# Sums by node in a graph kernel on Trainium2: one-hot matrices stationary instead of gathered rows, and row weights multiplied by ScalarE

## The chip, the cores and the metric

The kernel runs on one NeuronCore of a Trainium2 chip (trn2). The metric is the device time of the whole kernel in microseconds (us). Before the change the median of three runs is 7461.32 us (7460.88 to 7475.34).

## What is computed

The input is a graph of 12500 nodes with 256 features each and 212500 edges (200000 drawn ones and one loop for each node), sorted by destination. Four layers follow one another, each added to its input, each on the layer-normalized input: a relational graph sum, a feed-forward layer on the half of the nodes that a router scores highest, a graph attention sum with 4 heads of 64 columns, and a mixture of 8 experts of which each node takes two. The change is in the two sums. Cut to them:

```python
# relation sum (8 relations, block-diagonal weights 32x32)
msg = h[edge_src] * edge_norm[:, None]
agg = segment_sum(msg, edge_rel * N + edge_dst, num_segments=R * N)
out = einsum('rnbi,rbio->nbo', agg.reshape(R, N, 8, 32), W)
...
# attention sum
alpha = leaky_relu(a_src[src] + a_dst[dst], 0.2)
ex = exp(alpha - segment_max(alpha, dst)[dst])
w = ex / segment_sum(ex, dst)[dst]
agg = segment_sum(xp[src] * w[..., None], dst)
x = x + elu(agg.reshape(n, 256) + bias)
```

## The kernel before, in words

The kernel has one path for graphs whose edges lie evenly over the nodes, taken here (`even`, line 926), and a general path that is not run. The stages, with their stretches in the profile:

- **Preparation and table** (0 to 480 us). The edges are laid out in tiles of 128 (1661 tiles), their destinations are checked, and `lcC` gets each edge's destination relative to the first node of its tile's window. STEPS (line 299) fixes that first node for every tile t in advance: 16 times a step, moving by 241/512 of a step a tile, so about 7.5 nodes. A window is WIN = 96 nodes. Then every node's layer-normalized row times each of the 8 relations' weights is written to a table T0 in HBM, so that the relation sum needs only one row of 256 for each edge.
- **Relation sum and feed-forward** (480 to 2920 us, `even_depths`, line 936). For each tile GpSimd (POOL) gathers 128 rows of T0 with an indirect DMA (`gather`, line 233; buffers `row`, 16 of them). VectorE (DVE) makes a one-hot matrix S of 128 edges x 96 nodes for six tiles at once (`one_hot`, line 919) and multiplies it by the edge weights (line 1017). TensorE (PE) adds row-half x S into two banks of PSUM (`windows`, line 892; the matmul is line 913): the gathered half row, 128 edges x 128 features, is the stationary operand, S streams, and the sum comes out as features x nodes, 512 nodes to a bank ("bin"), features 0 to 127 in one bank and 128 to 255 in the other. A window that crosses the edge of a bin takes a matmul in each. When the last tile of a bin is through, `summed` (line 956) copies both banks (ScalarE one, DVE the other), transposes them back to nodes x features (PE, line 967), adds x, and goes on through layer norm, router score and feed-forward for these 512 nodes (lines 972 to 1009), in small pieces between the sums of the next nodes.
- **Choice of the top half and tables for the attention** (2920 to 3220 us).
- **Attention sum and router** (3220 to 6110 us, `even_gat`, line 1070). Rows of 260 (256 features and 4 scores) are gathered (`fetch`, line 1143; buffers of six tiles, 12 of them). For groups of 30 tiles (GS) the scores become softmax weights w (`scores`, `sources`, `softmax`, lines 1181 to 1244). DVE multiplies six tiles of rows by w at once (`weigh`, line 1249, instruction line 1253) and makes S (line 922). PE adds as before (line 913). `summed` (line 1109) does bias and ELU in features x nodes, transposes back (line 1128), adds the node's row, and `route` (line 673) normalizes, scores the experts, and scatters each node's row to its two experts' lists: 8 indirect DMAs on POOL for 512 nodes (line 740).
- **Experts** (6110 to 7439 us, `slots`, line 818). Not touched.

The order of PE, DVE, ScalarE (ACT) and SyncE (SP) instructions within the two sums is written out by a planner (class `Plan`, line 50). Step t is the step of tile t's gather. Each piece of work is put at a step, pieces of a step run in the order in which they were put, and a generator's `yield n` puts its next piece n steps later. In the relation sum S of six tiles is at t - 8 and the use at t + 3; in the attention sum S is at 12, `weigh` at 17 and the first use at 19 steps after the group's end. `queue` lets one block of nodes start only when the one before is through; `follow` doesn't wait. Every engine runs its list strictly in that order. POOL's gathers run ahead until no buffer is free.

Of the kernel before, what the change touches and what calls it, by code (L numbers as in the profile page):

```python
# [34 lines left out]
P = 128  # L36
# [8 lines left out]
BIN = 512  # L45
GS = 30
SUB = 6

# [52 lines left out]
def gnn_ffn_kernel(ctx: ExitStack, tc: tile.TileContext, x, src, dst, etype, eweight, w_rel, wr, br,  # L101
# [29 lines left out]
    def bcast(ap1d, n):  # L131
# [35 lines left out]
                   allow_small_or_imprecise_dtypes=True)  # L167
    ident = const.tile([P, P], F32, name="ident")
# [137 lines left out]

    def tiles_of(t):
        return t.rearrange("q (c j) -> q c j", j=P)
# [10 lines left out]
    with ExitStack() as pre:  # L319
# [63 lines left out]
        for i, (t, nat, around, dt) in enumerate(((NS, KSN, 0.0, F32), (NBR, NBN, -FAR, F32), (DM, DMN, 0.0, BF16))):  # L383
# [26 lines left out]
                                       accum_out=viol[:, 3:4])  # L410
        total = pp.tile([P, 1], F32, name="total")
# [240 lines left out]
    def router(st):  # L652
# [20 lines left out]
        def route(ms, xg, wk, pst, psy, psc, behind=None):  # L673
# [6 lines left out]
            xe = wk.tile([P, 4, D + 1], F32, name="xe", bufs=3)  # L680
# [66 lines left out]
            o = wk.tile([P, 4, D], F32, name="o")  # L747
            for i, m in enumerate(ms):
                pt = pst[0].tile([P, 2, P], F32, name=pst[1])
                transpose(pt[:NE, 0, :], mk[:, i, :])  # L750
                yield 1
                mT = wk.tile([NE, P], F32, name="mT")
                nc.scalar.activation(mT, pt[:NE, 0, :], AF.Copy)
                yield 1
                pb = psy[0].tile([P, D], F32, name=psy[1])
                nc.tensor.matmul(pb, mT, b2s, start=True, stop=True)
                yield 2
                nc.vector.tensor_tensor(o[:, i, :], pb, xg[:, i, :], op=OP.add)
                n = rows(m)
                nc.sync.dma_start(O2[m * P:m * P + n, :], o[:n, i, :])  # L760
# [131 lines left out]
    def windows(psA, done):  # L892


        zeros = const.tile([1, BIN], BF16, name="zeros")
        nc.vector.memset(zeros, 0.0)
        NBIN = -(-NM * P // BIN)
        last = {}
        for t in range(NT):
            for b in range(STEPS[t] * 16 // BIN, (STEPS[t] * 16 + WIN - 1) // BIN + 1):  # L900
                last[b] = t
        open_ = {}

        def add(t, lhs, S):
            base = STEPS[t] * 16
            for b in range(base // BIN, (base + WIN - 1) // BIN + 1):
                if b not in open_:
                    open_[b] = [psA.tile([P, BIN], F32, name=f"bin{k}") for k in range(2)]
                    for a in open_[b]:
                        nc.tensor.matmul(a, zeros[:, :P], zeros, start=True, stop=False)  # L910
                lo, hi = max(base, b * BIN), min(base + WIN, (b + 1) * BIN)
                for k in range(2):
                    nc.tensor.matmul(open_[b][k][:, lo - b * BIN:hi - b * BIN], lhs(k), S[:, lo - base:hi - base],  # L913
                                     start=False, stop=last[b] == t)
# [4 lines left out]
    def one_hot(wk, lcC, t, n, **kw):  # L919

        S = wk.tile([P, SUB, WIN], F32, name="S", **kw)
        nc.vector.tensor_tensor(S[:, :n], lcC[:, t:t + n, None].to_broadcast([P, n, WIN]),  # L922
                                col[:, None, :WIN].to_broadcast([P, n, WIN]), op=OP.is_equal)
        return S

    def even():
        with ExitStack() as ev:
# [3 lines left out]
            nc.sync.dma_start(lcC, LCC)  # L931
            even_depths(AD, lcC)
# [3 lines left out]
    def even_depths(AD, lcC):  # L936


        with ExitStack() as md:
# [8 lines left out]
            with ExitStack() as r1:  # L948
                wk = r1.enter_context(tc.tile_pool(name="r1_w", bufs=1))
                rw = r1.enter_context(tc.tile_pool(name="r1_r", bufs=16))  # L950
                psA = r1.enter_context(tc.tile_pool(name="r1_pa", bufs=2, space=PSUM))
# [3 lines left out]

                def summed(b, sums):
                    ms = [m for m in range(b * BIN // P, (b + 1) * BIN // P) if m < NM]
                    G = len(ms)
                    xg = wk.tile([P, 4, D], F32, name="xg")
                    load_nodes(xg, x, ms, nc.sync)  # L960
                    aT = wk.tile([P, 2, BIN], F32, name="aT")
                    nc.scalar.activation(aT[:, 0, :G * P], sums[0][:, :G * P], AF.Copy)
                    nc.vector.tensor_copy(aT[:, 1, :G * P], sums[1][:, :G * P])
                    yield 3
                    for i, m in enumerate(ms):
                        pt = pst.tile([P, 2, P], F32, name="pt")
                        for k in range(2):
                            transpose(pt[:, k, :], aT[:, k, i * P:(i + 1) * P])
                        yield 3
                        nc.vector.tensor_tensor(X[:, m, :], xg[:, i, :], pt.rearrange("p k j -> p (k j)"), op=OP.add)  # L970
# [40 lines left out]
                add = windows(psA, lambda b, sums: plan.queue(line, plan.now + 1, summed(b, sums)))  # L1011
                rows_, S_ = {}, {}

                def matrices(j):
                    n = min(SUB, NT - j * SUB)
                    S = one_hot(wk, lcC, j * SUB, n, bufs=4)
                    nc.vector.tensor_tensor(S[:, :n], S[:, :n],
                                            ewC[:, j * SUB:j * SUB + n, None].to_broadcast([P, n, WIN]), op=OP.mult)
                    S_[j] = S
# [4 lines left out]

                def use(t):
                    g = rows_.pop(t)
                    add(t, lambda k: g[:, k * P:(k + 1) * P], S_[t // SUB][:, t % SUB, :])

                for t in range(NT):
                    if t % SUB == 0:  # L1030
                        plan.put(t - 8, lambda j=t // SUB: matrices(j))
                    plan.put(t, lambda t=t: fetch(t))
                    plan.put(t + 3, lambda t=t: use(t))
# [36 lines left out]
    def even_gat(AD, lcC):  # L1070

        with ExitStack() as ga:
# [25 lines left out]
            psA = ga.enter_context(tc.tile_pool(name="ga_pa", bufs=2, space=PSUM))  # L1098
# [4 lines left out]
            biasC = wp.tile([P, 2, 2], F32, name="biasC")  # L1103
            nc.sync.dma_start(biasC[:, :, 0], bias.rearrange("(k p) -> p k", p=P))
            nc.vector.tensor_scalar(biasC[:, :, 1], biasC[:, :, 0], -1.0, None, op0=OP.mult)

            plan = Plan()

            def summed(b, sums):
                ms = [m for m in range(b * BIN // P, (b + 1) * BIN // P) if m < NM]  # L1110
                G = len(ms)
                xg = wk.tile([P, 4, D], F32, name="xg")
                load_nodes(xg, X2, ms, nc.sync)
                u = wk.tile([P, 2, BIN], F32, name="u", bufs=1)
                en = wk.tile([P, 2, BIN], F32, name="en", bufs=1)
                for k in range(2):
                    s_, e_ = sums[k][:, :G * P], en[:, k, :G * P]
                    nc.scalar.activation(e_, s_, AF.Relu, scale=-1.0, bias=biasC[:, k, 1:2])
                    nc.vector.tensor_scalar(u[:, k, :G * P], s_, biasC[:, k, 0:1], 0.0, op0=OP.add, op1=OP.max)
                    yield 1  # L1120
                nc.scalar.activation(en[:, :, :G * P], en[:, :, :G * P], AF.Exp, scale=-1.0)
                yield 2
                nc.vector.tensor_tensor(u[:, :, :G * P], u[:, :, :G * P], en[:, :, :G * P], op=OP.add)
                yield 2
                for i, m in enumerate(ms):
                    pt = pst.tile([P, 2, P], F32, name="pt")
# [553 lines left out]
```

## Time and profile before

| What | Value |
|---|---|
| Median of three runs | 7461.32 us |
| The profiled execution | 7440.8 us, of it 7439.0 from the first to the last instruction |
| Granted TensorE clock, mean over the span | 0.719 |
| PE busy | 5498.0 us (74%) |
| PE weight loads busy (PEld) | 4635.6 us (62%) |
| DVE busy | 2928.5 us (39%) |
| ACT busy | 745.9 us (10%) |
| POOL busy | 4095.7 us (55%) |

A line of the profile's groups has the kernel's line, the engine, the operation, output and inputs by name with their shapes, the count, then the busy time and the mean in ns of one, and then the engine's idle time just before them with what ended most of it. In the timeline the first two columns are the start and the duration in us. An f32 matmul stands in the trace as two instructions, so 7700 records of line 913 in each stage are 3850 matmuls. Ends of matmuls are modelled; starts are not.

### The profile page before, as it was taken

How to read it: one execution, taken by the hardware profiler on the slowest of the kernel's cores; microseconds unless marked ns; L12 is line 12 of the kernel's file. 1: busy time of each engine (PE TensorE's matmuls, PEld its weight loads, DVE VectorE, ACT ScalarE, POOL GpSimd, SP SyncE). 2: the span in 40 equal slices, each digit the busy share in tenths (PEclk: the TensorE clock that was granted, in tenths of full speed). 3: DMA queues.
4: the chain of work that ended last, by engine and by line, in shares of the span. 5: the costliest groups of instructions: out<-in, count | busy, mean ns of one | idle time of the engine just before them, and what ended most of it. 6: DMA issues, size and time to landing. Idle time of an engine off the chain costs nothing. (4 is left out here: it accounts for less than half of the span.)

```text
span 7439.0 us, 75728 instructions
## 1 busy us (share of the span) xinstructions
PE 5498.0 (74%) x26987; PEld 4635.6 (62%) x26987; DVE 2928.5 (39%) x7669; ACT 745.9 (10%) x1537; POOL 4095.7 (55%) x3768
## 2 busy tenths in 40 slices
PE   7967888887788887537777776767867775777775
PEld 3446667666677766427666676766766764666654
DVE  6633222323332222745556565565554650111110
ACT  2310000000000000110000000000000001112111
POOL 0036666666666664047777777777777742222222
PEclk9977787877778888765555555565555557888887
DMA  7753333333333332444444444444444425555555
GB/s 253 300 202 96 102 100 101 100 98 100 101 101 102 102 101 68 150 133 119 123 120 120 124 121 122 124 119 121 122 121 116 126 77 173 138 137 142 137 136 158
DMA packets 437371, 949.39 MB, mean 128 GB/s; under 512 B 84371, under 2 KB 293222, under 8 KB 410783
## 3 DMA queue, kind: packets, MB, share of 16 engines
q0 software_dynamic: 199872, 494.39, 25.6%
q1 hardware_dynamic: 237108, 450.03, 19.4%
q8 instruction: 217, 3.56, 0.2%
q14 instruction: 174, 1.42, 0.1%
HBM read 617.71 MB, written 228.88 MB: 114 GB/s over the span
## 5 line engine op out<-in xcount | busy, mean ns | idle before, releaser
L234 POOL DMA_INDIRECT rows<-T1A,srcC x1661 | 1867.0, 1124 | 684.0 <-issue 455.5
L234 POOL DMA_INDIRECT row<-T,rowC x1661 | 1655.5, 997 | 847.8 <-issue 327.2
L913 PE MATMUL bin<-S,rows 128*128 128x96 f32 (+5 forms) x7700 | 1724.1, 391 | 340.5 <-issue 235.6
L913 PEld LDWEIGHTS bin<-S,rows 128*128 128x128 f32 x7700 | 1604.1, 304 | 444.5 <-issue 315.6
L913 PEld LDWEIGHTS bin<-S,row 128*128 128x128 f32 x7700 | 1232.5, 241 | 237.4 <-issue 221.1
L913 PE MATMUL bin<-S,row 128*128 128x96 f32 (+5 forms) x7700 | 1248.7, 322 | 98.9 <-issue 94.0
L882 POOL DMA_INDIRECT O<-y,toI x210 | 326.7, 1556 | 907.0 <-DVE y L881 419.1
L872 PE MATMUL ph<-xT,we 128*128 128x256 f32 x1680 | 469.7, 442 | 267.7 <-DVE xT L191 262.8
L922 DVE TENSOR_TENSOR S<-lcC,col 128x576 f32<-128x576 f32 x554 | 415.9, 751 | 440.8 <-PE bin L913 175.8
L872 PEld LDWEIGHTS ph<-xT,we 128*128 128x128 f32 x1680 | 372.7, 227 | 344.0 <-DVE xT L191 275.6
L993 PE MATMUL ph<-xT,w1s 128*128 128x512 f32 (+1 forms) x800 | 426.1, 663 | 132.9 <-ACT hT L995 68.6
L1253 DVE TENSOR_TENSOR rows<-rows,w 128x1536 f32<-128x1536 f32 x277 | 484.8, 1750 | 79.6 <-issue 60.9
L861 DVE CAST toI<-xs 128x2 int32<-128x2 f32 x105 | 17.7, 169 | 1024.6 <-DMA O<-y,toI 820.9
L878 PE MATMUL py<-we,hT 128*128 128x256 f32 x1680 | 381.1, 379 | 5.7 <-DVE y L881 5.7
L1001 PE MATMUL pt<-w2s,hT 128*128 128x256 f32 x1568 | 378.5, 385 | 3.2 <-issue 3.1
L469 PE MATMUL pm<-BD,xT 128*128 128x512 f32 x784 | 351.1, 601 | 12.8 <-ACT xT L189 12.3
L878 PEld LDWEIGHTS py<-we,hT 128*128 128x128 f32 x1680 | 318.8, 190 | 50.9 <-DVE y L881 7.7
L195 PE MATMUL pt<-ident,xn 128*128 128x128 f32 x588 | 121.7, 317 | 289.1 <-DVE xn L219 176.0
L993 PEld LDWEIGHTS ph<-xT,w1s 128*128 128x128 f32 x800 | 153.9, 213 | 254.6 <-issue 180.4
L1001 PEld LDWEIGHTS pt<-w2s,hT 128*128 128x128 f32 x1568 | 284.7, 191 | 36.1 <-issue 4.5
L189 ACT ACTIVATE xT<-pt 128x256 f32<-128x256 f32 x301 | 115.2, 383 | 1840.2 <-PE pt L195 979.6
L195 PEld LDWEIGHTS pt<-ident,xn 128*128 128x128 f32 x588 | 79.9, 164 | 342.1 <-issue 317.2
(267 smaller groups left out, 4893.5 us busy)
## 6 DMA issues: line engine op xcount, KB each, us to landing
we<-Wall SPq DMA_DIRECT2D x105, 1026.0 KB
T<-tb SPq DMA_DIRECT2D x97, 1024.0 KB
dmB<-DMN SPq DMA_DIRECT2D x277, 192.0 KB
xs<-XS SPq DMA_DIRECT2D x105, 257.0 KB
row<-T,rowC POOLq DMA_INDIRECT x1661
rows<-T1A,srcC POOLq DMA_INDIRECT x1661
xg<-in_x_dram SPq DMA_DIRECT2D x48, 512.0 KB
T1A<-t SPq DMA_DIRECT2D x97, 130.0 KB
```

What stands on the lines that cost most here:

```text
L189: nc.scalar.activation(dst_ap, src_ap, AF.Copy)
L195: nc.tensor.transpose(o, i, ident[:k, :k])
L234: return nc.gpsimd.indirect_dma_start(out=o, out_offset=None, in_=table, in_offset=bass.IndirectOffsetOnAxis(ap=idx, axis=0))
L469: nc.tensor.matmul(pm, xT[:, k, :], BD[:, k, r4:r4 + 4, :], start=True, stop=True)
L872: nc.tensor.matmul(ph, we[:, k * EH + f * P:k * EH + (f + 1) * P], xT[:, k, :], start=k == 0, stop=k == 1)
L878: nc.tensor.matmul(py, hT[:, f, i * P:(i + 1) * P], we[:, A1 + f * D:A1 + (f + 1) * D], start=f == 0, stop=f == KE - 1)
L882: nc.gpsimd.indirect_dma_start(out=O2, out_offset=bass.IndirectOffsetOnAxis(ap=toI[:, i:i + 1], axis=0), in_=y, in_offset=None, compute_op ...
L913: nc.tensor.matmul(open_[b][k][:, lo - b * BIN:hi - b * BIN], lhs(k), S[:, lo - base:hi - base], start=False, stop=last[b] == t)
L922: nc.vector.tensor_tensor(S[:, :n], lcC[:, t:t + n, None].to_broadcast([P, n, WIN]), col[:, None, :WIN].to_broadcast([P, n, WIN]), op=OP.i ...
L993: nc.tensor.matmul(ph[:, :G * P], w1s[:, k, f * P:(f + 1) * P], xT[:, k, :G * P], start=k == 0, stop=k == 1)
L1001: nc.tensor.matmul(py, hT[:, f, i * P:(i + 1) * P], w2s[:, f, :], start=f == 0, stop=f == KH - 1)
L1253: nc.vector.tensor_tensor(r, r, group[g]["w"][:, o:o + c, :, None].to_broadcast([P, c, H, CH]), op=OP.mult)
```

## The change

- **Sums by node.** `windows` becomes `node_sums`. The stationary operand is now a one-hot matrix of 128 edges x 128 nodes, whole node tiles; the gathered row streams, all 256 columns in one matmul, and the sum comes out as nodes x features. A bank of PSUM holds two node tiles. MEETS lists the one or two node tiles that a tile's window touches; each takes a matmul. The preparation makes `lcC` relative to the first touched node tile, and `col2` holds 0 to 255 so that a second matrix compares with 128 to 255.
- **One-hot matrices** of 128 columns are made for three tiles (FEW) at a time, one instruction for the first node tile and one for each run of tiles that touch a second.
- **Weights.** In the relation sum S is no longer multiplied by the edge weights; ScalarE multiplies the gathered row (`scale`). In the attention sum ScalarE multiplies each tile's row, 64 columns of each head at a time, by w (`weigh`); DVE's multiplication of six tiles goes.
- **After a sum.** The sums need no transposing: x is added straight from PSUM for two node tiles, and layer norm and what follows start for four node tiles (`depths`; in the attention sum bias and ELU for two, `route` for four, one after another through `queue`). The node rows xg are loaded ahead (`nodes`) instead of when the bin is full.
- **Buffers.** row 16 to 15, banks for sums four to three, xe 3 to 2, o of one node tile instead of four, f, b and ex 2 to 1, xg 2 or 3.

The general path is as it was. The diff, cut to its core:

```diff
@@ preparation
+        into = pp.tile([P, C], I32, name="into")
+        nc.vector.tensor_copy(into, first)
+        nc.vector.tensor_scalar(into, into, P - 1, None, op0=OP.bitwise_and)
+        nc.vector.tensor_copy(first, into)
+        nc.vector.tensor_tensor(tiles_of(lc), tiles_of(lc), first[:, :, None].to_broadcast([P, C, P]), op=OP.add)
@@ windows -> node_sums
+    MEETS = [sorted({STEPS[t] * 16 // P, (STEPS[t] * 16 + WIN - 1) // P}) for t in range(NT)]
-        def add(t, lhs, S):
-            base = STEPS[t] * 16
-            for b in range(base // BIN, (base + WIN - 1) // BIN + 1):
...
-                lo, hi = max(base, b * BIN), min(base + WIN, (b + 1) * BIN)
-                for k in range(2):
-                    nc.tensor.matmul(open_[b][k][:, lo - b * BIN:hi - b * BIN], lhs(k), S[:, lo - base:hi - base],
-                                     start=False, stop=last[b] == t)
+        def add(t, row, S):
+            for k, m in enumerate(MEETS[t]):
+                b = m // 2
+                if b not in open_:
+                    open_[b] = psA.tile([P, 2, D], F32, name="bin")
+                    nc.tensor.matmul(open_[b].rearrange("p k d -> p (k d)"), zeros[:, :P], zeros,
+                                     start=True, stop=False)
+                nc.tensor.matmul(open_[b][:, m % 2, :], S(k), row, start=False,
+                                 stop=last[b] == t and m == max(n for n in MEETS[t] if n // 2 == b))
@@ one_hot
-        S = wk.tile([P, SUB, WIN], F32, name="S", **kw)
-        nc.vector.tensor_tensor(S[:, :n], lcC[:, t:t + n, None].to_broadcast([P, n, WIN]),
-                                col[:, None, :WIN].to_broadcast([P, n, WIN]), op=OP.is_equal)
+        S = [wk.tile([P, size, P], F32, name=f"S{k}", **kw)
+             for k in range(max(len(MEETS[t + i]) for i in range(n)))]
+        for k in range(len(S)):
...
+                    nc.vector.tensor_tensor(S[k][:, i:e], lcC[:, t + i:t + e, None].to_broadcast([P, e - i, P]),
+                                            col2[:, None, k, :].to_broadcast([P, e - i, P]), op=OP.is_equal)
@@ even_depths
-                    nc.scalar.activation(aT[:, 0, :G * P], sums[0][:, :G * P], AF.Copy)
-                    nc.vector.tensor_copy(aT[:, 1, :G * P], sums[1][:, :G * P])
...
-                            transpose(pt[:, k, :], aT[:, k, i * P:(i + 1) * P])
-                        yield 3
-                        nc.vector.tensor_tensor(X[:, m, :], xg[:, i, :], pt.rearrange("p k j -> p (k j)"), op=OP.add)
+                    nc.vector.tensor_tensor(X[:, ms[0]:ms[0] + n, :], xg_[b // 2][:, ms[0] % 4:ms[0] % 4 + n, :],
+                                            sums[:, :n, :], op=OP.add)
+                    if ms[-1] == quad_tiles(b // 2)[-1]:
+                        plan.queue(line, plan.now + 1, depths(quad_tiles(b // 2)))
...
-                    nc.vector.tensor_tensor(S[:, :n], S[:, :n],
-                                            ewC[:, j * SUB:j * SUB + n, None].to_broadcast([P, n, WIN]), op=OP.mult)
+                def scale(t):
+                    nc.scalar.activation(rows_[t], rows_[t], AF.Copy, scale=ewC[:, t:t + 1])
...
-                        plan.put(t - 8, lambda j=t // SUB: matrices(j))
-                    plan.put(t + 3, lambda t=t: use(t))
+                        plan.put(t - 4, lambda j=t // FEW: matrices(j))
+                    plan.put(t + 3, lambda t=t: scale(t))
+                    plan.put(t + 4, lambda t=t: use(t))
+                for q, t in OPENS.items():
+                    plan.put(t - 8, lambda q=q: nodes(q))
@@ even_gat
+                nc.vector.tensor_tensor(u, sums[:, :n, :], biasB[:, None, :].to_broadcast([P, n, D]), op=OP.add)
+                yield 1
+                nc.scalar.activation(en, u, AF.Relu, scale=-1.0)
+                nc.scalar.activation(en, en, AF.Exp, scale=-1.0)
+                yield 2
+                nc.vector.scalar_tensor_tensor(u, u, 0.0, en, op0=OP.max, op1=OP.add)
+                yield 1
+                nc.vector.scalar_tensor_tensor(xg_[q][:, i:i + n, :], u, -1.0, xg_[q][:, i:i + n, :],
+                                               op0=OP.add, op1=OP.add)
...
-                nc.vector.tensor_tensor(r, r, group[g]["w"][:, o:o + c, :, None].to_broadcast([P, c, H, CH]), op=OP.mult)
+            def weigh(t):
+                j, s = divmod(t, SUB)
+                g, o = divmod(t, GS)
+                for h in range(H):
+                    r = rows_[j][:, s, h * CH:(h + 1) * CH]
+                    nc.scalar.activation(r, r, AF.Copy, scale=group[g]["w"][:, o, h:h + 1])
...
-                        plan.put(t + GS + 12 + k * SUB, lambda j=j: matrices(j))
-                        plan.put(t + GS + 17 + k * SUB, lambda j=j: weigh(j))
+                        for i in range(2 * j, min(2 * j + 2, -(-NT // FEW))):
+                            plan.put(i * FEW + GS + 16, lambda i=i: matrices(i))
+                            plan.put(t + GS + 16 + k * SUB + s, lambda t=j * SUB + s: weigh(t))
                             plan.put(t + GS + 19 + k * SUB + s, lambda t=j * SUB + s: use(t))
```

## The prediction, made blind

> **What bounds the kernel now.** I read the page's first two parts, then the busy times of five stretches, the costliest groups, and last stretches of the timeline. The two stages that the change touches are the relation sum (480 to 2920 us) and the attention sum (3220 to 6110 us), 5330 us of 7439. In the two lines of stretches the columns are PE, PEld, DVE, ACT and POOL busy with counts, then granted clock, DMA share, GB/s.
>
> ```profile
> 480.00:2920.00 2440.00, 1951.23 (x10350) 1655.42 (x10349) 716.96 (x1657) 159.99 (x257) 1644.09 (x1650) 0.79 0.35 99
> ...
> 3220.00:6110.00 2890.00, 2054.62 (x10952) 1904.05 (x10950) 1559.07 (x3583) 136.57 (x331) 2076.61 (x1852) 0.55 0.45 118
> 6110.00:7439.00 1329.00, 903.04 (x3819) 749.21 (x3819) 148.53 (x505) 242.17 (x533) 353.86 (x238) 0.84 0.54 145
> ```
>
> ScalarE is nearly free in both stages, PE and POOL are not, and TensorE's clock is 0.55 in the second.
>
> ```profile
> L234 POOL DMA_INDIRECT rows<-T1A,srcC x1661 | 1867.0, 1124 | 684.0 <-issue 455.5
> L234 POOL DMA_INDIRECT row<-T,rowC x1661 | 1655.5, 997 | 847.8 <-issue 327.2
> ...
> L1253 DVE TENSOR_TENSOR rows<-rows,w 128x1536 f32<-128x1536 f32 x277 | 484.8, 1750 | 79.6 <-issue 60.9
> ```
>
> One gather's median is 953 ns in both stages (view of line 234), and the next one starts 0.30 us later ("0.30 <-issue" below): 1.257 us for a tile of 128 edges is the floor. 1661 x 1.257 = 2088 us. From the records of POOL's gathers:
> - Relation sum, first gather to last 2442 us: 1655 busy + 506 of 0.305 us gaps + 280 of longer pauses (230 of them), in which POOL waits for a row buffer that PE frees.
> - Attention sum, 2798 us: 1867 gathers + 197 scatters + 559 of 0.305 us gaps + 175 of longer pauses. So POOL is 94% taken, and a mean gather of 1124 ns instead of 953 costs 284 us. Laid against VectorE's records, 228 of these 284 us belong to 227 gathers that lie mostly beside L1253, as here:
>
> ```profile
> 4169.54 1.75 DVE L1253 TENSOR_TENSOR rows<-rows,w 128x1536 f32<-128x1536 f32 x1
> 4169.78 2.34 POOL L234 DMA_INDIRECT rows<-T1A,srcC  x1 [0.30 <-DVE f L1233]
> ...
> 4174.44 1.75 DVE L1253 TENSOR_TENSOR rows<-rows,w 128x1536 f32<-128x1536 f32 x1
> 4174.94 2.06 POOL L234 DMA_INDIRECT rows<-T1A,srcC  x1 [0.30 <-issue]
> ...
> 4177.31 0.95 POOL L234 DMA_INDIRECT rows<-T1A,srcC  x1 [0.30 <-issue]
> ```
>
> In the relation sum 61 of 73 us lie beside L1017, the multiplication of S by ewC. Both lines go.
>
> PE's price per instruction is read from starts in order (an f32 matmul is two instructions):
>
> ```profile
> 1542.09 1.03 PE L913 MATMUL bin<-S,row 128*128 128x96 f32 x8
> 1542.95 1.91 PE L993 MATMUL ph<-xT,w1s 128*128 128x512 f32 x4
> ...
> 1562.43 1.92 PE L1001 MATMUL pt<-w2s,hT 128*128 128x256 f32 x8
> 1564.19 0.58 PE L913 MATMUL bin<-S,row 128*128 128x96 f32 x4
> ```
>
> 96 columns: (1542.95 - 1542.09)/8 = 0.108 us; 256 columns: (1564.19 - 1562.43)/8 = 0.220. Over all records the medians are 0.112 and 0.216 at full clock; the first is 0.213 at half. 96, 48 and 16 columns cost the same 0.112[...].
>
> [...]2.34 and 2.06 us beside L1253, 0.95 alone. [...]of 1281 following pairs of L1001 in the relation sum (256 columns) every one lies at full clock, of 4937 of the 96-column ones of the attention sum 1070 do. [...]The trace has 383 ns for 256 from PSUM (L189), 687 for 512 with a bias pointer (L995): 170 and 260 ns beside the elements.
>
> **The change, part by part.**
>
> *PE, sums.* By STEPS (line 299) the 96-node window touches two node tiles in 1067 of 1661 cases, so 2728 matmuls of 256 columns for 3850 of up to 96. At full clock: 5456 x 0.216 = 1178 us for 7700 x 0.112 = 862: +316 in each stage. The 98 x 2 transposes back go in each: 196 x 0.11 = -21. Relation sum in all: 1178 + L993 800 x 0.429 = 343 + L1001 1568 x 0.216 = 339 + other transposes and rest 65 = 1925 us, before about 1630. Attention sum: 1178 + 230 (pad, px, route) = 1410, before about 1110. This is under POOL's time only if the clock rises. I take it that it does: half clock would make the sums alone 5456 x 0.427/1661 = 1.40 us a tile, full-width work without pause, and such work (L1001) is never at half; the last stage with its 256-column matmuls has 0.84 at 903 us busy of 1329. Bounds: 0.79/0.55 as now, and 1.0.
>
> *VectorE.* L1253 goes: -485 us, and L1017: 277 x 0.76 = -210. One-hot matrices: 277 x 0.75 = 208 us become 554 of 384 columns (0.55 us by the row of 576: 0.15 fixed + 0.4) and 420 of mean 325 (0.49): 510 us in each stage. None is on the path (717 and 1559 us busy of 2440 and 2890). What counts is POOL: -228 and -61 us of stretched gathers; the more numerous one-hots stretch others (now 21 and 5 us for 277; doubled, +22 and +10; bounds 0 and +60). In the preparation four operations, the largest 128x1664 (about 1.9 us): +3 us.
>
> *ScalarE, new in the path.* Relation sum: 1661 activations of 256 with a pointer, 0.26 + 0.21 = 0.47 us, 781 us beside 160. Attention sum: 4 x 1661 of 64 elements: 0.26 + 0.05 = 0.31 us each, 0.22 overlapped: 0.9 to 1.25 us a tile against POOL's 1.257 + scatters' 0.15. Hidden under POOL, but narrowly at the upper end. Queued behind a waiting multiplication are the Gelus (L995), mT, w and Exp; and behind a Gelu waiting for PE the next row. In the relation sum a multiplication is one step ahead of its use: after L993 PE does one tile (0.71 us) while ScalarE does Gelu (0.69) and the row (0.47), so PE waits some 0.5 us, 8 x 25 times: 100 us of PE, not of POOL while row buffers remain (15 x 1.26 = 19 us). In the attention sum the lead is three steps (4 us).
>
> *PE's waits in order.* In 700 to 2700 us PE waited 262 us for DVE xn, mv, xT, X and ACT hT: 13 us per 512 nodes. The layer-norm chain stays, waits for the transposed sums and their two-engine copy go: 9 us plus 4 of the new ScalarE waits. So 512 nodes (68 tiles) cost PE 1925/24.4 = 79 us + 13 = 92 at full clock; POOL 68 x 1.27 = 86; now 100. The relation sum is thus near balance, and pauses remain.
>
> *SyncE, POOL.* The same 25 loads of xg per stage on SP, issued earlier, into two and three buffers that the node tiles of two or three loads before left some 68 tiles ago: they wait for nothing, so nothing behind them on SP (dmB, masks, stores) does: 0; if one did wait, masks and dmB have 5 and 12 steps to spare. One small iota: under 1 us. Scatters as before, 196.
>
> *Sum* (profiled execution 7440.8, span 7439.0; the median of the runs is 7461.3, 20.5 more, kept):
> relation sum: stretched gathers -61 + 10, pauses 280 to about 220: -110. Attention sum: -228 + 22, pauses 175 to about 135: -246. Preparation +3, tails (49 tiles after the last gather at ScalarE's pace instead of half-clock PE's) +10. Together -343: 7440.8 - 343 = 7098; as a median 7461 - 343 = **7118**.
>
> **Rivals.**
> - *The clock doesn't follow* (ends slower). Place: PE in both stages. At 0.79 and 0.55 the relation sum takes 1925/0.79 + 220 waits = 2657 (+217), the attention sum 1410/0.55 + 350 waits (L1253, mT, transposes, in the trace) = 2914 (+24): 7461 + 241 + 13 = 7715. It decides when the relation sum's clock stays under some 0.80 while the attention sum's stays under 0.58. For: 0.79 and 0.55 now. Against: L1001, never at half. 0.14.
> - *ScalarE becomes the attention sum's bound*: 1.25 + 0.08 a tile + waits on PE and DVE of 0.3 (mT and ex wait long now, 346 and 290 us, but mostly because nothing else is there) = 1.63 x 1661 = 2707 + head and tail 90 = 2800 (-90); relation sum -80: 7461 - 160 = 7300. For: strict order. Against: overlap of neighbours. 0.16.
> - *Both stages fall to POOL's floor*, no pauses: -331 and -381: 6750 to 6920. Against: PE's 92 to POOL's 86, and scatters in POOL's queue that wait for the route. 0.08.
> That the matmuls don't change as said is no rival: the list of instructions has 2728.
>
> **How the numbers follow.** Forecast 0.62 (6920 to 7250), the others as above. Range 6920 to 7400: it leaves out the floor case (0.07) and the clock case (0.13). Within 0.2% (15 us, about what a measurement tells): 0.03, between ScalarE's case and the clock's. Faster 0.84, slower 0.13.
>
> **What would show it.** Right: gathers' mean in the attention sum under 1.02 us; clock there over 0.7; multiplications at 0.22 to 0.32 us; relation sum 2300 to 2380 us, attention sum 2580 to 2690. Wrong: gathers still at 1.1 us[...], clock at 0.55, or ScalarE busy over 85% of the attention sum.

## The result: slower, and the profile after

The changed kernel takes 7698.14 us (median of four runs, 7687.44 to 7701.77), the kernel before 7468.33 in the same comparison (four runs, 7460.88 to 7486.41): ratio 1.0302, 95% interval 1.0279 to 1.0325. The forecast was 7118 and faster. The profiled execution of the changed kernel is 7699.1 us, of it 7697.4 us span.

First the stretches of the profile after, with the columns of the stretches shown before: the relation sum, the attention sum, the experts.

```profile
480.00:3130.00 2650.00, 2112.16 (x7910) 1559.25 (x7910) 767.80 (x2012) 883.90 (x1889) 1630.76 (x1657) 0.89 0.32 92
...
3430.00:6370.00 2940.00, 1911.42 (x8524) 1412.42 (x8522) 1357.25 (x4013) 1747.60 (x7001) 1881.12 (x1858) 0.78 0.44 117
6370.00:7697.00 1327.00, 900.35 (x3803) 748.38 (x3803) 141.26 (x466) 241.95 (x529) 349.29 (x232) 0.84 0.54 144
```

The relation sum is 210 us longer (2650 for 2440), the attention sum 50 (2940 for 2890), the experts the same. The granted clock did rise, from 0.79 to 0.89 and from 0.55 to 0.78. The costliest groups of the same profile:

```profile
L236 POOL DMA_INDIRECT row<-T,rowC x1661 | 1636.3, 985 | 1075.0 <-issue 336.9
L236 POOL DMA_INDIRECT rows<-T1A,srcC x1661 | 1684.9, 1014 | 937.1 <-issue 516.8
L919 PE MATMUL bin<-rows,S 128*128 128x256 f32 x5456 | 1681.7, 451 | 333.4 <-issue 215.6
...
L1285 ACT ACTIVATE rows<-rows,w 128x64 f32<-128x64 f32 x6644 | 1639.6, 344 | 105.1 <-issue 97.6
```

The gathers of the attention sum did become faster, 1014 ns for 1124. What took their gain is the idle time before them: 937.1 us for 684.0, and 1075.0 for 847.8 in the relation sum. Split as in the prediction (from the start of the first gather to the start of the last, from POOL's records; a pause is what a gap has above the usual 0.305 us):

| | first to last | mean gather | pauses |
|---|---|---|---|
| relation sum before | 2441 us | 997 ns | 280 us |
| relation sum after | 2649 us | 985 ns | 508 us |
| attention sum before | 2797 us | 1124 ns | 175 us |
| attention sum after | 2851 us | 1014 ns | 429 us |

+208 and +54 us, with -4 for everything else, are the 258 us between the spans (7697.4 - 7439.0).

What a pause looks like in the timeline after (start, duration, and in brackets the idle time before with what ended it):

```profile
1480.19 2.76 PE L919 MATMUL bin<-row,S 128*128 128x256 f32 x12
...
1482.13 0.40 DVE L221 TENSOR_SCALAR xn<-X,mv 128x256 f32<-128x256 f32 x1
...
1482.79 0.38 PE L197 MATMUL pt<-ident,xn 128*128 128x128 f32 x2
...
1487.24 0.96 POOL L236 DMA_INDIRECT row<-T,rowC  x1 [0.30 <-issue]
1490.84 0.39 ACT L191 ACTIVATE xT<-pt 128x256 f32<-128x256 f32 x1 [14.38 <-remote]
1490.88 0.76 DVE L949 TENSOR_TENSOR S<-lcC,col 128x384 f32<-128x384 f32 x2 [8.35 <-remote]
1491.12 2.10 ACT L1053 ACTIVATE row<-row,ewC 128x256 f32<-128x256 f32 x5
...
1491.67 2.93 PE L919 MATMUL bin<-row,S 128*128 128x256 f32 x6 [8.50 <-ACT row L1053]
```

TensorE is through with its sums at 1482.95 and with a transpose at 1483.17. ScalarE, which needs a transpose, and VectorE, which needs a buffer for its next matrices that TensorE has used, start only 7.7 us later, within 0.04 us of each other, and the trace names no releaser ("remote"). TensorE then waits for ScalarE, and POOL for TensorE. No engine is busy to full here; at this stop a signal came late. The trace records the semaphore increments by which TensorE signals: in these sums they should come every 0.43 us (two records, whose starts lie 0.216 us apart in the median), but here they come at 1484.43, 1485.85 and 1488.65 and then, from 1490.75 to 1491.14, eleven of them 0.03 to 0.05 us apart. ScalarE and VectorE start within that burst. The kernel before had such stops too: in its relation sum no matmul ran for over 4 us at some 40 places (about 270 us), in the changed kernel's at as many. Only a few of them end with a burst like this one; that late signals made the others is inferred.

These stops belong to a condition of the run, not of one kernel: where the kernel before takes 7340 to 7490 us every kernel's trace shows them (the "first kind" below, the recorded result among them), and where it takes 6950 to 7010 us waits of this sort are absent (the "second kind"); two chips showed both.

### The profile page after: what moved, and what is told of

Same layout as the page of the kernel before. It is cut to its first block, busy times and chain, and to the rows that moved or that the text cites. A ratio compares the mean times of both kernels' runs of the same rounds, so it can differ in the third digit from the quotient of the medians.

```text
span 7697.4 us, 78475 instructions
## 1 busy us (share of the span) xinstructions
PE 5511.6 (72%) x22105; PEld 4047.3 (53%) x22105; DVE 2770.5 (36%) x8412; ACT 3083.1 (40%) x9840; POOL 3876.8 (50%) x3769
## 5 line engine op out<-in xcount | busy, mean ns | idle before, releaser
L236 POOL DMA_INDIRECT row<-T,rowC x1661 | 1636.3, 985 | 1075.0 <-issue 336.9
L236 POOL DMA_INDIRECT rows<-T1A,srcC x1661 | 1684.9, 1014 | 937.1 <-issue 516.8
L919 PE MATMUL bin<-rows,S 128*128 128x256 f32 x5456 | 1681.7, 451 | 333.4 <-issue 215.6
L919 PE MATMUL bin<-row,S 128*128 128x256 f32 x5456 | 1489.0, 416 | 317.3 <-ACT row L1053 148.0
L1285 ACT ACTIVATE rows<-rows,w 128x64 f32<-128x64 f32 x6644 | 1639.6, 344 | 105.1 <-issue 97.6
L949 DVE TENSOR_TENSOR S<-lcC,col 128x384 f32<-128x384 f32 (+2 forms) x1948 | 956.1, 527 | 1947.8 <-PE bin L919 1085.4
L919 PEld LDWEIGHTS bin<-rows,S 128*128 128x128 f32 x5456 | 1132.2, 224 | 640.8 <-issue 334.5
L919 PEld LDWEIGHTS bin<-row,S 128*128 128x128 f32 x5456 | 1102.9, 208 | 687.6 <-issue 257.0
L1053 ACT ACTIVATE row<-row,ewC 128x256 f32<-128x256 f32 x1661 | 763.7, 504 | 757.6 <-DMA row<-T,rowC 642.0
L882 ACT ACTIVATE hT<-ph,we 128x256 f32<-128x256 f32 x420 | 199.5, 475 | 672.2 <-PE ph L880 672.2
L1024 PE MATMUL ph<-xT,w1s 128*128 128x512 f32 (+1 forms) x800 | 380.7, 602 | 0.7 <-DVE xT L193 0.7
L1026 ACT ACTIVATE hT<-ph,b1s 128x512 f32<-128x512 f32 (+1 forms) x200 | 135.8, 679 | 597.1 <-PE ph L1024 435.4
```

Of the source, the lines that this page charges most:

```text
L236: return nc.gpsimd.indirect_dma_start(out=o, out_offset=None, in_=table, in_offset=bass.IndirectOffsetOnAxis(ap=idx, axis=0))
L882: nc.scalar.activation(hT[:, f, :], ph, AF.Gelu, bias=we[:, A2 + f:A2 + f + 1])
L919: nc.tensor.matmul(open_[b][:, m % 2, :], S(k), row, start=False, stop=last[b] == t and m == max(n for n in MEETS[t] if n // 2 == b))
L949: nc.vector.tensor_tensor(S[k][:, i:e], lcC[:, t + i:t + e, None].to_broadcast([P, e - i, P]), col2[:, None, k, :].to_broadcast([P, e - i, ...
L1024: nc.tensor.matmul(ph[:, :G * P], w1s[:, k, f * P:(f + 1) * P], xT[:, k, :G * P], start=k == 0, stop=k == 1)
L1053: nc.scalar.activation(rows_[t], rows_[t], AF.Copy, scale=ewC[:, t:t + 1])
```

## The experiments

All figures of a sum are first gather to last (us) / mean gather (ns) / pauses (us), as in the table above. The lead is the number of steps from a row's multiplication to its use; a ring is a set of buffers used in turn.

**Both kernels where signals are prompt.** No edit.

> The kernel before, unchanged, beside the changed one on one chip: in the four experiments so far it took 6995 us where it had taken 7461 to 7486, and no POOL issue gap was over 0.3 us where before there were gaps of 2.7 us. Theory late signals (in the first two traces TensorE's semaphore increments reach the others late and in bursts; waits marked remote): here no bursts and about 7000 us, relation sum about 2230 us, attention sum about 2600. If it takes 7460 again without bursts, the difference of 466 us is of another kind (memory or clock).

> The changed kernel, unchanged. Theory late signals (they cost it more, since each of its matmuls signals and its rings are two to four steps deep): where no bursts are seen it takes 6790 to 6880 us and is 1.5 to 3% faster than the kernel before, with pauses of POOL in the relation sum near 200 us. Theory of the kernel's own waits (S ring, ScalarE's order, TensorE's work): it stays slower than the kernel before, 7050 us or more, where that takes 6995.

Measured: the kernel before 6969.5 us (one run, profiled) and 6976 in the comparison (seven runs); the changed kernel 6801.5 us (four runs), ratio 0.975 (0.9722 to 0.9779). The stretches and gathers of the kernel before, then of the changed one:

```profile
480.00:2650.00 2170.00, 2053.40 (x10367) 1702.22 (x10367) 716.76 (x1660) 162.03 (x260) 1655.04 (x1651) 0.78 0.38 112
...
2950.00:5600.00 2650.00, 2035.73 (x10723) 1892.35 (x10723) 1528.74 (x3501) 129.09 (x314) 2087.61 (x1850) 0.55 0.48 128
```

```profile
L234 POOL DMA_INDIRECT rows<-T1A,srcC x1661 | 1880.3, 1132 | 511.9 <-issue 441.1
L234 POOL DMA_INDIRECT row<-T,rowC x1661 | 1665.5, 1003 | 567.3 <-issue 258.8
```

```profile
480.00:2650.00 2170.00, 1973.44 (x7765) 1458.01 (x7766) 748.64 (x1953) 898.30 (x1859) 1602.93 (x1626) 0.97 0.38 111
...
2950.00:5600.00 2650.00, 1847.63 (x8814) 1399.23 (x8814) 1406.02 (x4237) 1739.93 (x7058) 1918.78 (x1886) 0.82 0.51 140
```

```profile
L236 POOL DMA_INDIRECT row<-T,rowC x1661 | 1639.0, 987 | 640.9 <-issue 242.7
L236 POOL DMA_INDIRECT rows<-T1A,srcC x1661 | 1691.2, 1018 | 511.9 <-issue 437.0
```

The kernel before: 2171 / 1003 / 0 and 2635 / 1132 / 3. Its relation sum is at POOL's floor: 1660 x (1.003 + 0.305) = 2171 us. So the 280 and 175 us of pauses in its first profile are not its own. The changed kernel: 2217 / 987 / 74 and 2432 / 1018 / 3. The attention sum gains 203 us, the relation sum loses 46. The waits that POOL's gathers stood in show the kinds apart; columns are the sum in us, the count, the longest. In the kernel before, recorded run, then the second kind:

```profile
POOL rows L234 <- issue: 455.5, 1485, 2.7
...
POOL row L234 <- PE bin L913: 265.9, 382, 6.2
```

```profile
POOL rows L234 <- issue: 441.1, 1448, 0.3
...
POOL row L234 <- PE bin L913: 165.5, 543, 0.3
```

Where no gap is longer than 0.3 us, nothing but the usual step lies between gathers. The changed kernel's 74 us of pauses in the relation sum remain in this kind: they are its own.

**What costs the changed kernel 46 us in the relation sum (second kind).** Three edits of it: rings (one-hot matrices made nearer to their use in the relation sum, and two steps earlier with five buffers in the attention sum); a lead longer by three steps; no matmul for a second node tile (these edges' parts are then missing in the sums). A fourth, `both`, has the first two edits (the matrices at t + 2 in the relation sum and GS + 17 in the attention sum, to stay 5 steps ahead).

```diff
# loose_S
-  plan.put(t - 4, lambda j=t // FEW: matrices(j))          # relation sum
+  plan.put(t - 1, lambda j=t // FEW: matrices(j))
-  ... bufs=3), matrices at i * FEW + GS + 16               # attention sum
+  ... bufs=5), matrices at i * FEW + GS + 14
# lead
-  plan.put(t + 4, lambda t=t: use(t))
+  plan.put(t + 7, lambda t=t: use(t))
-  plan.put(t + GS + 19 + k * SUB + s, lambda t=j * SUB + s: use(t))
+  plan.put(t + GS + 22 + k * SUB + s, lambda t=j * SUB + s: use(t))
# one_tile
-  for k, m in enumerate(MEETS[t]):
+  for k, m in enumerate(MEETS[t][:1]):
```

> The changed kernel (7698 us) with looser rings of one-hot matrices: in the relation sum they are written 5 steps ahead of their use instead of 8, so that their buffers must be free of a use 5 steps earlier instead of 2; in the attention sum five buffers instead of three. Theory S (VectorE hangs on TensorE's uses of the matrices, 738 us of waits in 2000, and so its layer norms come late and TensorE waits for them): the stretch of the relation sum falls from 2650 to about 2450 us, that of the attention sum from 2940 to about 2850, the whole to about 7400. Theories of ScalarE's order and of TensorE's own work: VectorE's waits shrink, each stretch moves by less than 40 us, the whole 7650 to 7720.

> The changed kernel with three steps more between ScalarE's multiplication of a row and TensorE's use of it (4 instead of 1 in the relation sum, 6 instead of 3 in the attention sum). Theory ScalarE (a multiplication stands in ScalarE's order behind a Gelu that waits for TensorE, so the next row comes late, 0.5 us and more every second tile): TensorE's and POOL's waits for the multiplication (L1053, L1285) mostly go, the relation sum falls from 2650 to about 2500 us, the attention sum from 2940 to about 2850; whole about 7460. Theory TensorE's work (full-clock time and lost clock are what fills the relation sum): under 50 us off the relation sum. Theory S: none.

> The changed kernel without the matmul of the second node tile, wherever a tile's window touches two (1067 of 2728 matmuls are left out, the one-hot matrices are still made): the sums lack these edges' parts. Full-clock TensorE work falls by 1067 x 0.43 = 460 us in each stage, to below that of the kernel before. Theory TensorE's work: the relation sum falls to about 2300 us and the attention sum to about 2750. Theory ScalarE or S: the waits between engines fill in what the matmuls leave, the relation sum stays above 2500 us, the attention sum above 2850.

> The changed kernel with the three steps more between multiplication and use and the looser rings of one-hot matrices together (matrices 5 steps ahead of their use in both stages, five buffers in the attention sum). If the two are separate waits, POOL's pauses in the relation sum fall below those of either (each alone gave 2225 and 2149 us from the first gather to the last): 2120 to 2140, whole 6710 to 6740. If they are one and the same slack, no gain over the longer lead alone: 6745 to 6765.

Relation sums: `loose_S` 2225 / 986 / 83, `lead` 2149 / 980 / 16, `one_tile` 2130 / 978 / 1, `both` 2141 / 985 / 0. In all, 6792, 6755 and 6715 us (one run each) beside 6995 for the kernel before, and `both` 6725 beside 6976 (0.9644, 0.9618 to 0.967). Rings alone make no difference; the lead does. What it ends is seen in the group of the sums, changed kernel (second kind) and then `lead`:

```profile
L919 PE MATMUL bin<-row,S 128*128 128x256 f32 x5456 | 1404.6, 398 | 135.7 <-ACT row L1053 132.6
```

```profile
L919 PE MATMUL bin<-row,S 128*128 128x256 f32 x5456 | 1349.6, 394 | 39.8 <-ACT row L1053 36.9
```

In ScalarE's order the next row's multiplication stands behind a Gelu that waits for TensorE; these waits (L1026 for L1024) fall as well, from 446 to 224 us. Without the second matmuls TensorE waits for the row far longer (308 us in `one_tile`), yet POOL has pauses of 1 us: it takes both, the dearer sums and the short lead. The attention sums are 2417 to 2432 in all four: there neither decides.

**The weights alone on ScalarE.** The kernel before with windows of 96:

```diff
-  nc.vector.tensor_tensor(S[:, :n], S[:, :n], ewC[...].to_broadcast([P, n, WIN]), op=OP.mult)
+  nc.scalar.activation(rows_[t], rows_[t], AF.Copy, scale=ewC[:, t:t + 1])
-  nc.vector.tensor_tensor(r, r, group[g]["w"][:, o:o + c, :, None].to_broadcast([P, c, H, CH]), op=OP.mult)
+  for h in range(H):
+      nc.scalar.activation(r, r, AF.Copy, scale=group[g]["w"][:, o, h:h + 1])   # r: 64 columns of one tile
```

> The kernel before (sums in windows of 96, gathered halves stationary) with the weights alone moved to ScalarE as in the changed kernel: the edge weights by one multiplication of 256 columns, the attention weights by four of 64. Theory TensorE's work (the loss is the 316 us of dearer matmuls in each stage): gathers fall to a mean of 0.99 to 1.02 us, the relation sum takes 2350 to 2400 us (before 2440), the attention sum 2600 to 2700 (before 2890), the whole about 7150 to 7250. Theory ScalarE (its place in the order costs the pauses): gathers faster as well, but the relation sum 2500 to 2600, the attention sum 2850 or more, the whole 7450 to 7650.

Second kind: 6728.6 us, ratio 0.9613 (0.9591 to 0.9635); 2153 / 980 / 20 and 2406 / 1006 / 3. So moving the weights is enough for all of the change's gain, and the new form of the sums costs 1.4% of the time (0.975 for 0.9613), with the longer lead and the rings 0.3% (`both`, 0.9644). With the longer lead (`use` at t + 7), and `both` again, both of the first kind:

> The kernel before with the weights alone on ScalarE, and in the relation sum three steps more between multiplication and use (4 instead of 1). On a chip where the kernel before takes about 6980: relation sum 2130 to 2140 us from first to last gather (2153 with the short lead), whole 0.958 to 0.961 of the kernel before, the best so far. On a chip where the kernel before takes about 7460: the theory of TensorE's dearer matmuls (this kernel has the cheap ones) gives 7150 to 7300; the theory that signals and instructions cost there (6644 more on ScalarE) gives POOL's pauses in the attention sum over 350 us and the whole 7400 to 7700.

> The changed kernel with the longer lead and the looser rings. Where the kernel before takes 6980: 0.964 again. Where it takes 7460: if the loss there is late signals meeting rings and leads that are one to four steps deep, the slack covers part of it: relation sum 2400 to 2550 us (changed kernel 2649), attention sum 2700 to 2800 (2851), whole 7250 to 7500. If each signal or instruction costs engine time by itself, slack doesn't help: relation sum 2600 or more, whole 7620 to 7720.

`act_lead` 7483 us beside 7374, ratio 1.0153 (1.0113 to 1.0192): 2464 / 983 / 327 and 2826 / 1006 / 419. `both` again 7517, 1.0205 (1.016 to 1.0249): 2467 / 983 / 330 and 2857 / 999 / 454. TensorE's dearer matmuls aren't needed for a loss: the kernel with the cheap ones and fast gathers is 1.5% slower too. Slack brings the relation sum to 2467, not to a gain, and the attention sum, expected at 2700 to 2800, stays at 2857.

**Weights back on VectorE.** The changed kernel with the six-tile multiplication of the kernel before in the attention sum (277 instructions for 6644):

```diff
-  plan.put(t + GS + 16 + k * SUB + s, lambda t=j * SUB + s: weigh(t))    # four of 64 columns
+  plan.put(t + GS + 17 + k * SUB, lambda j=j: weigh(j))                  # as in the kernel before
```

> The changed kernel with the attention weights multiplied as before the change, six tiles at once by VectorE (277 instructions instead of ScalarE's 6644). On a chip as in the last seven runs (kernel before near 6980): gathers stretched again beside the multiplication (mean 1.12 to 1.14 us instead of 1.018), the attention sum 190 to 210 us longer than the changed kernel's 2432 from first to last gather, the whole about 7000. On a chip as in the first two traces (kernel before 7461): the theory that there every record of an instruction or a signal costs[...] gives an attention sum shorter than the changed kernel's 2851, 2650 to 2750, in spite of the stretched gathers; the theory that TensorE's work or the order sets it there gives 2900 or more.

First kind: 7664.6 us beside 7459.8 (one run each); 2655 / 983 / 517 and 2795 / 1141 / 126. The attention sum lies between the two expectations.

```profile
L236 POOL DMA_INDIRECT rows<-T1A,srcC x1661 | 1895.4, 1141 | 635.1 <-issue 453.3
```

Against the changed kernel's attention sum, pauses fell by 303 us and the gathers' busy time rose by 210. I read this at first as ScalarE's instructions costing 300 us. The next edits overturn that.

**w in PSUM.** VectorE multiplies six tiles at once, but reads w where the transpose left it, so that only one input is in SBUF. That two inputs in SBUF are what stretches a gather was a guess up to here. `few_ps` is `both` with this (in the attention sum the uses stay at 19 steps and the matrices are at 14); `win_ps` is the kernel before with it, and with the edge weights put in by the comparison:

```diff
-  w = wk.tile([P, GS, H], F32, name="w")
-  nc.scalar.activation(w.rearrange("p t h -> p (t h)"), pw[:, :K], AF.Copy)
-  group[g]["w"] = w
+  group[g]["w"] = wP[:, g % 2, :K].rearrange("p (t h) -> p t h", h=H)    # wP: a PSUM tile
# win_ps only, for each tile of the six
+  nc.vector.tensor_scalar(S[:, i], col[:, :WIN], lcC[:, t:t + 1], ewC[:, t:t + 1], op0=OP.is_equal, op1=OP.mult)
```

> The changed kernel with the lead and the rings of the run both, and with the attention weights multiplied by VectorE six tiles at once, but with w left in PSUM, so that the multiplication has one input in SBUF instead of two. [...]gathers' mean in the attention sum 0.99 to 1.03 us, as with ScalarE, instead of 1.14; theory that any long VectorE operation stretches them: 1.12 to 1.14. Time[...]: where the kernel before takes about 6980, 0.963 to 0.967 of it (attention sum 2420); where it takes 7370 to 7460, POOL's pauses in the attention sum fall to about 130 us (few) with fast gathers, attention sum 2560 to 2640, whole 0.965 to 0.985, faster than the kernel before on both kinds of chip. If ScalarE's 6644 instructions are not what costs there, pauses stay over 350 us.

> The kernel before (windows of 96) with w left in PSUM in the same way, and with the edge weights put into the one-hot matrix by one instruction a tile (compare and multiply with two columns as scalars) in place of two for six tiles; ScalarE gets no new work. [...]gathers 0.98 and 1.01 us; where the kernel before takes 6980, 0.960 to 0.964 of it; where it takes 7370 to 7460, pauses of the attention sum 100 to 180 us and of the relation sum 280 to 330, whole 0.955 to 0.975 of the kernel before. If the comparison with scalars stretches gathers itself, the relation sum's mean is over 1.03 us.

Second kind: `few_ps` 0.9634 (0.9615 to 0.9654), 2139 / 984 / 0 and 2431 / 1015 / 3. `win_ps` 6666.7 us, ratio **0.954** (0.9523 to 0.9557), 2095 / 957 / 0 and 2398 / 1000 / 3: ahead of both kernels, with ScalarE given no new work. Two repeats of this kind gave 0.9548 and 0.9557; in the first of these comparisons the changed kernel took 6810 beside 6988 and `one_tile` 6730. The groups of `win_ps`:

```profile
L234 POOL DMA_INDIRECT rows<-T1A,srcC x1661 | 1660.9, 1000 | 512.1 <-issue 426.6
L234 POOL DMA_INDIRECT row<-T,rowC x1661 | 1590.2, 957 | 567.2 <-issue 281.3
...
L1254 DVE TENSOR_TENSOR rows<-rows,px 128x1536 f32<-128x1536 f32 x277 | 483.8, 1747 | 124.9 <-PE px L1217 119.4
```

The multiplication lasts as long as before, 1747 ns, and hardly stretches the gathers any more: their mean is 1000 ns, for 1132 in the kernel before of this kind.

**The same where signals are late.** `split` has one edit in each stage of the changed kernel: second matmuls left out in the relation sum alone; w in PSUM on VectorE, and five buffers of matrices, in the attention sum (the edits shown above).

```diff
-  add = node_sums(psA, lambda b, sums: ...)                      # relation sum
+  add = node_sums(psA, lambda b, sums: ..., [m[:1] for m in MEETS])
```

> The changed kernel with one edit in each stage. Relation sum: the second node tile's matmuls are left out (these edges' parts are missing), lead and rings as changed. Attention sum: all matmuls, weights multiplied by VectorE with w in PSUM, five buffers of one-hot matrices; ScalarE has no multiplications. Kernel before at 7370 to 7490: relation sum 2300 to 2450 us from first to last gather if TensorE's work decides it there, 2550 or more if lead and rings do; attention sum 2560 to 2640 with pauses under 200 if ScalarE's multiplications are what costs, over 2750 if late signals cost any form as much. Kernel before at 6980: 2130 and 2430.

> As the run before it. Kernel before at 7370 to 7490: savings on gathers turn into pauses: 0.985 to 1.005 of the kernel before, pauses 300 to 400 us in each sum; POOL's gathers set the end: 0.95 to 0.965. Kernel before at 6980: 0.955.

First kind: `split` took 7420.8 us beside 7380.4 (one run each): 2490 / 992 / 338 and 2745 / 1010 / 329. Its relation sum lies between the two expectations, its attention sum just under what was expected if late signals cost any form as much. `win_ps` took 7465.2 beside 7375.8, ratio 1.0106 (1.0074 to 1.0137), a little above the 1.005 that was expected at most: 2415 / 959 / 317 and 2843 / 993 / 458. Its gathers:

```profile
L234 POOL DMA_INDIRECT rows<-T1A,srcC x1661 | 1649.3, 993 | 967.3 <-issue 444.0
...
L234 POOL DMA_INDIRECT row<-T,rowC x1661 | 1593.3, 959 | 884.1 <-issue 346.4
```

Against `win_ps` above, busy times are equal to 1% and the idle time before the attention's gathers goes from 512.1 to 967.3 us. Without ScalarE's 6644 instructions and with fast gathers the pauses are 329 and 458 us, with them 419 to 454: not more than some 100 us can be put down to them. In this kind the attention sum takes 2745 to 2857 us in all seven traces, whether a mean gather takes 0.99 or 1.14 us, whoever multiplies, and whichever way the sums are formed.

## Why the prediction was wrong, step by step

- **Stretched gathers: right; what the one-hot matrices add: too small.** "-228 and -61 us of stretched gathers", with +22 and +10 for the more numerous one-hots: the gathers' busy time fell by 182 us in the attention sum (means 1124 to 1014 ns), for 206 forecast, and by 19 in the relation sum (997 to 985), for 51. With each gather's excess over 953 ns laid to the VectorE instruction that lies beside it longest, the one-hot matrices went from 21 and 5 us to 54 and 42. In the second kind the attention sum gained 203 us for the 206 of the sum (-228 + 22), with pauses of 3 us on both sides. That it is VectorE's second input in SBUF which stretches a gather was not shown before the result; for this multiplication `few_ps` and `win_ps` show it, since with one of its inputs in PSUM a mean gather takes 1.015 and 1.000 us (1.132 in the kernel before of that kind and 1.141 in `few`, with both in SBUF).
- **The failed step: "pauses 280 to about 220 (relation), 175 to about 135 (attention)", and with it that a shorter gather shortens the stage.** Measured: 508 and 429. I took POOL, "94% taken", for the bound of the attention sum and its pauses for waits on TensorE's queue. In the condition of the recorded runs POOL was not the bound: it ran ahead and waited for buffers, and, as far as the stop above and the second kind show, for signals that came late. The attention's gathers gave 182 us (1867.0 to 1684.9) and the pauses took 254. So the relation sum, forecast at -110 us, measured +208, and the attention sum, forecast at -246, +54. `win_ps` shows it bare: gathers of the attention sum faster by 131 ns, 218 us in all, pauses up by 283 (175 to 458). Where signals are prompt the kernel before has no pauses that could shrink, and the change saves about 175 us (6976 to 6801) of the 343 forecast: the forecast took pauses for the kernel's own that were not.
- **TensorE's price: right; its waits: mis-sized for this condition.** The sums' matmuls start 0.216 us apart at full clock, as forecast (median, 0.427 at half). At such prices the matmuls from first gather to last of the relation sum come to some 1850 us, for a predicted 1925 with the tail. "13 us per 512 nodes" makes 317 us in all. Counted from starts, an estimate: about 300 us idle in the second kind, but some 630 in the recorded run, and over 500 already in the kernel before there. I had counted only the waits with a named releaser (262 us of 2000) and left out what stood under "remote" and "issue". That was the term of the sum for which the trace had the evidence.
- **The extra 208 us of the relation sum in the first kind** seem to come where TensorE's added work meets short slack: leaving out the second matmuls (2490) or giving lead and rings (2467) each takes most of it. The comparisons differ by some 90 us for the kernel before itself (7468 and 7375), so the share of each is known only roughly.
- **Clock: right** (0.89 and 0.78; 0.97 and 0.82 with prompt signals), though its evidence was put too strongly: of the pairs of L1001 in the relation sum before, 1281 of 1288 were at full clock, not all. What sets the granted clock was not shown; that it would rise with full-width work was my estimate from these pairs. The rival "the clock doesn't follow" ended near the measured time, 7715, for a reason that did not happen.
- **ScalarE as the attention's bound: refuted in the second kind.** 0.334 us an instruction, overlapped to 1613 / 1661 = 0.97 a tile, against a pace of 2432 / 1661 = 1.46 us; the sums waited 83.6 us for it in all. The times that the forecast worked with are in the trace of before: 383 and 597 ns for 256 and 512 elements from PSUM (L189), 474 and 687 with a bias pointer (L995), so 0.83 ns an element; the overlap of neighbours is in the trace of after, where an instruction of L1285 lasts 344 ns and adds 1639.6 / 6644 = 0.247 us.
- **The lead: mechanism right, reach wrong.** "100 us of PE, not of POOL while row buffers remain" became 133 us of TensorE's waits for the row and 74 us of POOL's pauses in the second kind; 37 and 16 with the longer lead.
- **The rest: small, as said.** Preparation and tails were put at +13 us; all that lies outside the two sums measured -4. A one-hot instruction of 384 columns takes 554 ns, for 0.55 us forecast.

**What stays open** is why signals are late. Instruction records are as many in both kinds (75,728 in the kernel before), but of its semaphore updates 47,603 are recorded in the first kind and 97,825 in the second. So a wait under "remote" can also be one whose signal left no record; that the waits are real is shown by the longer time, not by that name. Instructions and updates together come to 14 to 19 a microsecond in both sums of all seven traces of the first kind, to 27 to 33 in the two kernels' traces of the second; in the last 1100 us both kinds record the same, 16. That the recording itself makes the stops was a guess of mine; no run here shows it or tells it from a slow path of the signals. What would bound the attention sum at 2745 to 2857 us is open with it.

## What to carry to other kernels

Before a saving on the busiest engine is booked as time, ask what ends its pauses: if there are waits under "remote", or gaps far above the engine's usual one (2.7 us where 0.3 is usual), that engine may not be the bound, and what it saves can turn into more pause, as it did here. Take a second trace of the same kernel in another run before the sum is made; here one of the second kind showed the pauses to be foreign. To free a GpSimd gather from a VectorE multiplication, it was enough here to leave the small operand in PSUM (mean gather 1000 ns in `win_ps`, 1132 in the kernel before).

## What the hardware showed that I had not expected

- The same program ran 7% apart (6970 and 7461 us) with gather times (1003 and 997 ns) and granted clock (0.716 and 0.719) nearly equal: as far as the profile shows, the difference lies in waits.
- A VectorE operation of 1747 ns with one input in PSUM hardly touches the gathers (277 of them stretch gathers by 4 us in `win_ps`, by 22 in `few_ps`), where the same with both in SBUF (1750 ns) stretches them by 239 us in the kernel before of the second kind.
- A comparison and multiplication with two columns as scalars, 96 wide, takes 349 ns and hardly stretches the gathers (mean 957 ns, for a median of 953).
